# Folding the third hop's weights into the first hop's, and turning its sums on VectorE

## The chip, the core and the metric

The kernel runs on one core of a Trainium2 chip. The metric is device time in microseconds; the time before is the median of three runs. A core has five engines that run side by side, each with its own queue of instructions in order: TensorE (matrix products; PE in the profile, with its weight loads as PEld), VectorE (DVE), ScalarE (ACT), GpSimd (POOL) and SyncE (SP, which here issues the loads). Products land in PSUM banks, and VectorE or ScalarE copies them out.

## The reference

Four layers over one graph of 3327 nodes with 64 features. Each layer takes a layernorm and a relu of `x`, propagates over the dense matrix `adj`, and adds its result to `x`. Cut to what matters:

```
# layer 0: two gated steps                         (hops 0 and 1, adj)
h = relu(layernorm(x));  x = x + L0(h, adj)
# layer 1: out = w @ (h @ weight) + bias           (hop 2, w from the ranks of adj's entries)
h = relu(layernorm(x));  x = x + L1(h, adj)
# layer 2: w = adj * adj                           (hops 3, 4, 5)
h = relu(layernorm(x))
t = h
for W, b in ((W0, b0), (W1, b1), (W2, b2)):
    t = w @ t
    t = t @ W.T + b
x = x + t
# layer 3: twice                                   (hops 6 and 7, adj)
h = relu(layernorm(x));  t = h
for k in range(2):
    t = tanh(concatenate([adj @ t, t], axis=1) @ W[k])
x = x + t
```

## The kernel before, in words

The nodes are padded to 26 blocks of 128, kept as two halves of 13 blocks. The 13 blocks form four chunks (`CH`): chunks 0, 1 and 2 have three blocks (384 columns), chunk 3 has four (512 columns). A chunk stands for its blocks in both halves. Chunks 0 and 1 are group 0, chunks 2 and 3 group 1. A tile is one row block of `adj.T` (128 source nodes) with the columns of one group in both halves; it is loaded by SP into one of 20 slots.

A *unit* (`propagate`, L613) multiplies one tile with the features of its source block, for one destination chunk, and adds to that chunk's sums in PSUM: features stand in the first half of the partitions for the first half of the nodes, in the second for the other. Products in float32 appear as two records each, so that a unit has four.

`joint(g, k, sweep, later, keep)` runs hop k and hop k+1 for group g over the same loaded tiles. First come the tiles whose sources lie in the other group; hop k+1 follows hop k by `later` tiles. Then come the group's own twelve (or fourteen) tiles for hop k alone: all but the last `sweep` for both chunks at a time, then the last `sweep` for the first chunk, then the same ones for the second. When a chunk's sums are complete, its task `after_k` is begun. Then hop k+1 takes the waiting tiles (`keep`), then the tiles whose sources lie in the group's first chunk, for which that chunk's new features must be ready, then those of the second chunk.

Everything is emitted by one Python program in a manual order. The tasks are generators: `yield 1.2` hands back until units of about that many microseconds have been emitted (`spend`). The order of instructions on each engine is the order of emission, and the engines wait for each other's results. If a unit needs features that are not emitted yet (`finish`), the rest of that task is emitted at once.

For hops 3 to 5 the matrix is squared element by element, on ScalarE (L446) or VectorE (L448). `square` gives every third square to VectorE, but none while any chunk's task is open (`ch in tasks`). In hops 3 and 4 the square replaces the tile where it lies. In hop 5 the tile is needed unsquared for hop 6, so `expand` writes the square into half a slot, at most three units ahead of the unit in hand.

Layer 2 in the kernel before: `fold_hops` computes, from the weights in `bd` (index 0 is layer 1's weight, 1 to 3 are W0, W1, W2 transposed, each twice on a block diagonal) and the biases in `brow`, the product of the first two weights (`product(1, 2)`, L214), the first bias carried through the second weight (L241) and the second bias as a column (`hopcol`, L242). Then
- `after_3` copies the sums (`evacuate`, L759 on ScalarE or L761 on VectorE), multiplies with the folded weight (`dense_to_nodes`, recorded at L313, which also turns features into node rows) and adds the folded bias (L1005);
- `after_4` copies the sums with the second bias added (`sums_to_nodes`, L816, ScalarE) and turns them into node rows with VectorE's 32x32 block transposes, sixteen a chunk (L825);
- `after_5` copies the sums, multiplies with W2 (L313), adds the result to `x` (`xs`, L865), takes the layernorm (L843 to L858, with one step on GpSimd at L854) and leaves a feature copy for hop 6 (`transpose_on_vector`, L809);
- the third bias is added to `x` in `after_2`, 15 us after the layernorm (`add_row`, L871).

`after_6` copies the sums into the stacked buffer `both` (`evacuate_stacked`: first half L830 on ScalarE, second half L834 on VectorE), multiplies with layer 3's weights (L780), and ScalarE takes the tanh (L1030).

Of the kernel before, what the change touches and what calls it, by code (L numbers as in the profile page):

```python
# [9 lines left out]
F32 = mybir.dt.float32  # L10
# [3 lines left out]
ALU = mybir.AluOpType  # L14
# [30 lines left out]
N, D = 3327, 64  # L45
P = 128
# [8 lines left out]
CWM = 512  # L55
GROUPS = [(0, 1), (2, 3)]
# [9 lines left out]
WL1, WL2, WL3 = 14, 15, 18  # L66
# [25 lines left out]
def upper(n):  # L92
    return slice(n * D, (n + 1) * D)
# [3 lines left out]
def kernel(  # L97
# [9 lines left out]
    nc = tc.nc  # L107
# [3 lines left out]
    work = ctx.enter_context(tc.tile_pool(name="work", bufs=4))  # L111
# [99 lines left out]
        nc.scalar.copy(ahead[c], ps[:, :width(c)])  # L211
        give(i)

    def product(i, j):  # L214

        n, ps = take()
        mm(ps[:, :P], bd[:, i, :], ident)
        tr = work.tile([P, P], F32, name="t2")
        nc.scalar.copy(tr, ps[:, :P])
        give(n)  # L220
        yield 1.0
        n, ps = take()
        mm(ps[:, :P], tr, bd[:, j, :])
        nc.scalar.copy(bd[:, i, :], ps[:, :P])
        give(n)
        yield 1.0

    def fold_hops():

        i, ps = take()  # L230
        for n in range(3):
            for h in range(2):
                nc.tensor.matmul(ps[upper(h), n * P:(n + 1) * P], brow[:, n], ident, start=True, stop=True)
        cols = work.tile([P, CWM], F32, name="t2")
        nc.scalar.copy(cols[:, :3 * P], ps[:, :3 * P])
        give(i)
        yield 1.0

        i, ps = take()
        mm(ps[:, :D], cols[:, :P], bd[:, 2, :D])  # L240
        nc.vector.tensor_copy(brow[:, 0], ps[:, :D])  # L241
        nc.vector.tensor_copy(hopcol[:, 0:1], cols[:, P:P + 1])  # L242
        give(i)
        yield 1.0
        yield from product(1, 2)

    def more_constants():
        nc.gpsimd.memset(cells, 0.0)
# [59 lines left out]
    def mm(out, lhsT, rhs, start=True, stop=True):  # L308


        for h in range(2):
            hs = slice(h * D, (h + 1) * D)
            nc.tensor.matmul(out[hs], lhsT[:, hs], rhs, start=start, stop=stop)  # L313
# [8 lines left out]
    def take(sums=False, either=True):  # L322


        either = either and not sums
        pool = idle_sums if sums else idle_temps
        if either and idle_sums and (not pool or released[idle_sums[0]] < released[pool[0]]):
            pool = idle_sums
        for c in list(tasks):
            if not pool and c not in running:  # L330
                advance(c)
        i = pool.popleft()
        return i, banks[i]

    def give(i):
        released[i] = max(released) + 1
        (idle_sums if i < 4 else idle_temps).append(i)

    def nodes(c):

        return feat.tile([P, blocks(c), 2, D], F32, name=f"y{c}")

    def flat(t):
        return t.rearrange("p b s d -> p b (s d)")
# [4 lines left out]
    def xchunk(c):  # L349
        return xs[:, CH[c][0]:CH[c][1]]  # L350
# [21 lines left out]
    def finish(c):  # L372
        while c in tasks:
            advance(c)
# [286 lines left out]
    def joint(g, k, sweep, later, keep, lag=None):  # L661


        a, b = GROUPS[g]
        in_place = KIND[k] != PLAIN and KIND[k + 1] == SQUARED
        early = (KIND[k], KIND[k + 1]) == (PLAIN, RANKED)
        waiting = deque()
        counting = Counting(g, lag)

        def both(t):  # L670
            for c in (a, b):
                put(k, c, t)
            if lag is not None:
                counting.add(t)

        def second(n):
            for _ in range(n):
                if waiting:
                    t = waiting.popleft()
                    for c in (a, b):  # L680
                        put(k + 1, c, t)

        for q in sources_of(*GROUPS[1 - g]):
            t = Tile(q, g, in_place, early)
            both(t)
            waiting.append(t)
            if len(waiting) > later:
                second(1)
        own = [[Tile(q, g, in_place, early) for q in sources_of(c)] for c in (a, b)]
        all_own = own[0] + own[1]  # L690
        for n, t in enumerate(all_own[:-sweep]):
            both(t)
            second(len(waiting) + n + 1 > later if early else min(2, len(waiting) - keep))
        counting.rest()
        for c in (a, b):
            for t in all_own[-sweep:]:
                put(k, c, t)
                if lag is not None and c == a:
                    counting.add(t)
            if KIND[k] == RANKED:  # L700
                units.append((k, c, SPECIAL))
        counting.rest()
        second(len(waiting))
        for t in own[0]:
            for c in (a, b):
                put(k + 1, c, t)
        for c in (a, b):
            for t in own[1]:
                put(k + 1, c, t)
            if KIND[k + 1] == RANKED:  # L710
                units.append((k + 1, c, SPECIAL))
# [44 lines left out]
    def evacuate(acc, c, busy=False):  # L756
        m = work.tile([P, CWM], F32, name="t2")[:, :width(c)]
        if c % 2 or busy:
            nc.scalar.copy(m, acc[0][1][:, :width(c)])  # L759
        else:  # L760
            nc.vector.tensor_copy(m, acc[0][1][:, :width(c)])  # L761
        give(acc[0][0])
        return m

    def dense_to_nodes(ft, w, c):

        i, ps = take()
        v = view(ps, c)
        for b in range(blocks(c)):
            mm(v[:, b, :], ft[:, b * P:(b + 1) * P], bd[:, w - WL1, :])  # L770
        return i, v
# [38 lines left out]
                if q % 2:  # L810
                    yield 1.5

    def sums_to_nodes(acc, c, bias):

        m = work.tile([P, CWM], F32, name="t2")[:, :width(c)]
        nc.scalar.activation(m, acc[0][1][:, :width(c)], AF.Identity, bias=hopcol[:, bias:bias + 1])  # L816
        give(acc[0][0])
        yield 0.8
        v = m.rearrange("p (b q n) -> p b q n", q=4, n=32)
        yk = nodes(c)  # L820
        for s in range(2):
            for f in range(2):
                at = s * D + f * 32
                for q in range(4):
                    nc.vector.transpose(yk[q * 32:(q + 1) * 32, :, s, f * 32:(f + 1) * 32], v[at:at + 32, :, q])  # L825
                yield 1.2
        return yk

    def evacuate_stacked(acc, c, on_scalar=False):
        nc.scalar.copy(both[c][upper(0), 0], acc[0][1][upper(0), :width(c)])  # L830
        if on_scalar:
            nc.scalar.copy(both[c][upper(1), 1], acc[1][1][upper(1), :width(c)])
        else:
            nc.vector.tensor_copy(both[c][upper(1), 1], acc[1][1][upper(1), :width(c)])  # L834
        for i in {acc[0][0], acc[1][0]}:
            give(i)
# [24 lines left out]
    def residual(v, c, relu=False):  # L861
        if relu:
            nc.vector.scalar_tensor_tensor(flat(xchunk(c)), v[1], 0.0, flat(xchunk(c)), op0=ALU.max, op1=ALU.add)
        else:
            nc.vector.tensor_tensor(flat(xchunk(c)), flat(xchunk(c)), v[1], ALU.add)  # L865
        give(v[0])

    def add_row(c, i):

        n = 2 * blocks(c)  # L870
        nc.vector.tensor_tensor(groups(xchunk(c)), groups(xchunk(c)),  # L871
                                brow[:, i:i + 1, :].to_broadcast([P, n, D]), ALU.add)
# [113 lines left out]
    def after_2(c, acc):  # L986
        m = evacuate(acc, c)
        yield 1.4
        v = dense_to_nodes(m, WL1, c)
        yield 1.2  # L990
        residual(v, c)
        yk = nodes(c)
        yield from layernorm_relu(yk, c, squares_on_scalar=c in GROUPS[0])
        y[3][c] = yk
        yield 15.0
        add_row(c, 2)

    def after_3(c, acc):
        m = evacuate(acc, c)
# [11 lines left out]
        y[5][c] = yield from sums_to_nodes(acc, c, 0)  # L1011

    def after_5(c, acc):
        m = evacuate(acc, c)
        yield 0.8
        v = dense_to_nodes(m, WL2 + 2, c)
        yield 0.8
        residual(v, c)
        yk = nodes(c)
        yield from layernorm_relu(yk, c)  # L1020
        y[6][c] = yk
        yield 8.0
        yield from transpose_on_vector(yk, c)

    def after_6(c, acc):
        evacuate_stacked(acc, c)
        yield 1.3
        v = stacked_to_nodes(c, lambda s: w3[:, 0, s])
        yk = nodes(c)
        nc.scalar.activation(flat(yk), v[1], AF.Tanh)  # L1030
        give(v[0])
        y[7][c] = yk
        yield 8.0
        yield from transpose_on_vector(yk, c)
# [20 lines left out]
    joint(1, 2, sweep=6, later=6, keep=1)  # L1055
    joint(0, 3, sweep=8, later=4, keep=4)
    joint(1, 4, sweep=8, later=4, keep=4)
    joint(0, 5, sweep=8, later=4, keep=4)
    joint(1, 6, sweep=8, later=4, keep=4)
    alone(0, 7, sweep=6, parts=True)  # L1060

# [55 lines left out]
```

## Time and profile before

| | |
|---|---|
| median of three runs | 697.64 us (697.54 to 697.74) |
| the profiled execution's own time | 697.73 us |
| its span in the profile | 695.7 us |
| instructions in it | 12589 |
| GpSimd busy | 77.8 us (11%) |
| loads and stores | 201.31 MB, mean 289 GB/s |
| mean granted TensorE clock | 0.999 |

Engine shares name the busy time of each engine, its share of the span and its instructions. A group of instructions has the line, the engine, the operation, what it writes and reads, and the count. In the list of waits a row says who waited for whom: microseconds in total, times, the longest. The chain of waits is the work that ended last, followed back from the end. In the timeline a row has start, duration, engine and line; the bracket gives the idle time before it and what ended that.

### The profile page before, as it was taken

The numbers are of one execution on the slowest core, as the hardware profiler recorded it, in microseconds if no ns is written. First come the engines' busy times: TensorE is split into PE (matmuls) and PEld (weight loads), VectorE is DVE, ScalarE is ACT, GpSimd is POOL, SyncE is SP. The second block draws the span as 40 slices with busy tenths as digits, with TensorE's granted clock in tenths as the row PEclk, the third lists the DMA queues.
The fourth block names the chain that finished last, engine by engine and source line by source line (L and its number), as shares of the span: only waits on it lengthen the run. The fifth ranks groups of instructions, "written<-read, shape, count | busy, mean of one in ns | idle before, by whom it ended". The sixth has DMA issues, their size and how long they took to land.

```text
span 695.7 us, 12589 instructions
## 1 busy us (share of the span) xinstructions
PE 681.0 (98%) x5072; PEld 380.4 (55%) x5072; DVE 355.3 (51%) x772; ACT 274.3 (39%) x426; POOL 77.8 (11%) x114
## 2 busy tenths in 40 slices
PE   7899999999999999999999999999999999999997
PEld 4686667645566785556444444343344444344587
DVE  5946745755997899757341106325271565005101
ACT  1013000403147878888998107722176500000101
POOL 5300000002480414111100000000000000000000
PEclk9999999999999999999999999999999999999999
DMA  9999998099879921792899569954997399917991
GB/s 341 401 400 406 403 407 274 1 349 389 277 242 376 317 96 60 259 316 80 311 361 351 206 216 409 404 227 131 396 370 264 110 399 405 405 75 268 404 403 65
DMA packets 68693, 201.31 MB, mean 289 GB/s; under 512 B 7244, under 2 KB 8372, under 8 KB 68636
## 3 DMA queue, kind: packets, MB, share of 16 engines
q1 hardware_dynamic: 65724, 199.08, 76.9%
q10 hardware_dynamic: 736, 1.23, 0.5%
q8 instruction: 40, 0.66, 0.4%
q0 software_dynamic: 2176, 0.20, 0.2%
q14 instruction: 17, 0.14, 0.0%
HBM read 199.45 MB, written 0.85 MB: 288 GB/s over the span
## 4 chain that ended last, share of the span: by engine, by line
PE 58%; DVE 1%; ACT 0%; POOL 0%; issue 0%; DVEq 0%; ACTq 0%; POOLq 0%
PE sum L613 54%; PE temp L313 3%; PE temp L780 1%; ACT e L529 0%; POOL st L854 0%; DVE both L834 0%; DVE e L527 0%; PE sum L313 0%; ACT both L830 0%; DVE y L858 0%; DVE y L850 0%; DVE t L845 0%; DVE st L851 0%; DVE st L843 0%; DVE xs L865 0%
## 5 line engine op out<-in xcount | busy, mean ns | idle before, releaser
L613 PE MATMUL sum<-adj,y 128*64 128x384 f32 (+3 forms) x3016 | 535.4, 501 | 1.5 <-DVE y L858 0.7
L613 PEld LDWEIGHTS sum<-adj,y 128*64 128x64 f32 x3016 | 248.8, 137 | 230.5 <-issue 196.9
L446 ACT ACTIVATE adj<-adj 128x768 f32<-128x768 f32 (+1 forms) x176 | 144.4, 892 | 45.9 <-PE sum L613 23.0
L472 DVE TENSOR_SCALAR adj<-adj 128x768 bf16<-128x768 f32 (+3 forms) x208 | 114.0, 597 | 32.6 <-PE temp L548 24.7
L613 PE MATMUL sum<-e,both 128*64 128x384 bf16 (+1 forms) x624 | 74.0, 339 | 0.5 <-DVE e L527 0.5
L529 ACT ACTIVATE e<-temp,bitsb 128x384 int16<-128x384 f32 (+1 forms) x120 | 67.8, 607 | 14.9 <-PE temp L313 9.1
L830 ACT COPY both<-sum 64x384 f32<-64x384 f32 (+3 forms) x17 | 8.1, 478 | 148.2 <-PE sum L613 148.2
L834 DVE COPY both<-sum 64x384 f32<-64x384 f32 (+3 forms) x13 | 7.3, 561 | 99.5 <-ACT both L830 98.9
L448 DVE TENSOR_TENSOR adj<-adj 128x768 f32<-128x768 f32 (+1 forms) x32 | 30.6, 1004 | 51.9 <-DMA adj<-in_adjT 33.1
L854 POOL TENSOR_TENSOR st<-st,mhalf 128x6 f32<-128x6 f32 (+1 forms) x16 | 24.9, 1553 | 287.8 <-DVE st L852 287.8
L313 PE MATMUL temp<-adj,tri 128*64 128x384 bf16 (+1 forms) x332 | 51.7, 341 | 1.3 <-ACT e L529 0.8
L613 PEld LDWEIGHTS <-both 128*64 128x64 bf16 x624 | 41.9, 110 | 18.3 <-issue 6.5
L477 POOL DMA_DIRECT2D adj<-totals x52 | 33.6, 648 | 52.6 <-PE temp L313 41.7
L313 PEld LDWEIGHTS <-tri 128*64 128x64 bf16 x416 | 29.2, 110 | 17.3 <-issue 9.8
L527 DVE TENSOR_SCALAR e<-temp 128x384 int16<-128x384 f32 (+1 forms) x46 | 28.3, 615 | 20.0 <-PE temp L313 9.6
L809 DVE STREAM_TRANSPOSE both<-y 32x96 f32<-32x96 f32 (+1 forms) x128 | 35.6, 278 | 2.9
L548 PE MATMUL temp<-adj,behind 128*64 128x384 bf16 x208 | 33.8, 340 | 2.8 <-DVE adj L472 2.6
L825 DVE STREAM_TRANSPOSE y<-t 32x96 f32<-32x96 f32 (+1 forms) x64 | 17.8, 278 | 24.7 <-ACT t L816 23.9
L548 PEld LDWEIGHTS <-behind 128*64 128x64 bf16 x208 | 20.8, 110 | 17.4 <-issue 13.5
L761 DVE COPY t<-sum 128x384 f32<-128x384 f32 x6 | 3.3, 555 | 35.7 <-PE sum L613 35.7
L186 ACT COPY t<-temp 128x128 f32<-128x128 f32 x1 | 0.3, 266 | 48.2 <-PE temp L184 48.2
L570 POOL MEMSET adj<- 128x768 f32 (+1 forms) x2 | 1.6, 800 | 133.2 <-PE sum L613 133.2
(132 smaller groups left out, 353.8 us busy)
## 6 DMA issues: line engine op xcount, KB each, us to landing
adj<-in_adjT SPq DMA_DIRECT2D x130, 768.0 KB, 9.0
adj<-in_adjT SPq DMA_DIRECT2D x104, 896.0 KB, 12.0
xs<-in_x ACTq DMA_DIRECT2D x1, 448.0 KB
adj<-totals POOLq DMA_DIRECT2D x26, 3.0 KB, 4.9
adj<-totals POOLq DMA_DIRECT2D x26, 3.5 KB, 2.3
out<-xs ACTq DMA_DIRECT2D x1, 256.0 KB
xs<-in_x SPq DMA_DIRECT2D x1, 192.0 KB
xs<-in_x ACTq DMA_DIRECT2D x1, 192.0 KB, 3.3
```

The lines of the kernel that those rows point to most:

```text
L313: nc.tensor.matmul(out[hs], lhsT[:, hs], rhs, start=start, stop=stop)
L446: nc.scalar.activation(sq, v, AF.Square)
L448: nc.vector.tensor_tensor(sq, v, v, ALU.mult)
L472: nc.vector.tensor_scalar(t.mask.view[:rows, half], t.view()[:rows, half], 0.0, None, op0=ALU.not_equal)
L477: nc.gpsimd.dma_start(out=t.mask.view[P - 1:P], in_=totals[t.g][t.q:t.q + D + 1:D, :])
L527: nc.vector.tensor_scalar(wide[:, s], ps[:, :w], BITS, 0.0, op0=ALU.add, op1=ALU.max)
L529: nc.scalar.activation(wide[:, s], ps[:, :w], AF.Relu, bias=bitsb)
L548: nc.tensor.matmul(counts[c][1][s * D:(s + 1) * D, :w], behind[:, NQ - 1 - t.q:NQ - 1 - t.q + D], t.mask.view[:, s, t.cols(c)], start=firs ...
L613: nc.tensor.matmul(acc[h][1][h * D:(h + 1) * D, :w], yq[h], rhs[h], start=first and n == 0, stop=last and n == len(terms) - 1)
L809: nc.vector.transpose(to[at:at + 32, :, q], h[q * 32:(q + 1) * 32, :, s, f * 32:(f + 1) * 32])
L825: nc.vector.transpose(yk[q * 32:(q + 1) * 32, :, s, f * 32:(f + 1) * 32], v[at:at + 32, :, q])
L854: nc.gpsimd.tensor_tensor(st[:, 3, :n], st[:, 2, :n], mhalf[:, :n], ALU.pow)
```

## The change

The three weights of layer 2 are folded into one before hop 3. With M the squared matrix, M(M(M h W0' + b0)W1' + b1)W2' + b2 is computed as M(M(M h W0'W1'W2' + b0 W1'W2') + b1 W2') + b2. The fold is done in three steps. After hop 5 the sums are copied with b2 added and turned on VectorE, as after hop 4; the second chunk of a group turns only after the first chunk's layernorm has been emitted (`behind`). `add_row(c, 2)` and the 15 us before it are gone. The `sweep` of hop 5 in group 0 grows from 8 to 12 tiles, and for group 0 both halves of the sums of hop index 6 are copied by ScalarE.

```diff
-    def product(i, j):
-
-        n, ps = take()
-        mm(ps[:, :P], bd[:, i, :], ident)
-        tr = work.tile([P, P], F32, name="t2")
-        nc.scalar.copy(tr, ps[:, :P])
-        give(n)
-        yield 1.0
-        n, ps = take()
-        mm(ps[:, :P], tr, bd[:, j, :])
-        nc.scalar.copy(bd[:, i, :], ps[:, :P])
-        give(n)
-        yield 1.0
-
     def fold_hops():
 
         i, ps = take()
-        for n in range(3):
+        for n, w in enumerate((P, 1, 1)):
             for h in range(2):
-                nc.tensor.matmul(ps[upper(h), n * P:(n + 1) * P], brow[:, n], ident, start=True, stop=True)
-        cols = work.tile([P, CWM], F32, name="t2")
-        nc.scalar.copy(cols[:, :3 * P], ps[:, :3 * P])
+                nc.tensor.matmul(ps[upper(h), (0, P, P + 1)[n]:(0, P, P + 1)[n] + w], brow[:, n], ident[:, :w],
+                                 start=True, stop=True)
+        for n in (1, 2):
+            mm(ps[:, (n + 1) * P:(n + 2) * P], bd[:, n, :], ident)
+        turns = work.tile([P, 4, P], F32, name="t2")
+        nc.scalar.copy(turns[:, 0:3].rearrange("p n f -> p (n f)")[:, :P + 2], ps[:, :P + 2])
+        nc.scalar.copy(turns[:, 2:4], ps[:, 2 * P:].rearrange("p (n f) -> p n f", f=P))
         give(i)
         yield 1.0
-
-        i, ps = take()
-        mm(ps[:, :D], cols[:, :P], bd[:, 2, :D])
-        nc.vector.tensor_copy(brow[:, 0], ps[:, :D])
-        nc.vector.tensor_copy(hopcol[:, 0:1], cols[:, P:P + 1])
+        i, ps = take()
+        mm(ps[:, :P], turns[:, 3], bd[:, 3, :])
+        mm(ps[:, P:P + 1], bd[:, 3, :], turns[:, 1, 0:1])
+        nc.scalar.copy(bd[:, 2, :], ps[:, :P])
+        nc.vector.tensor_copy(hopcol[:, 0:1], ps[:, P:P + 1])
+        nc.vector.tensor_copy(hopcol[:, 1:2], turns[:, 1, 1:2])
         give(i)
         yield 1.0
-        yield from product(1, 2)
+        i, ps = take()
+        mm(ps[:, :P], turns[:, 2], bd[:, 2, :])
+        mm(ps[:, P:P + D], turns[:, 0], bd[:, 2, :D])
+        nc.scalar.copy(bd[:, 1, :], ps[:, :P])
+        nc.vector.tensor_copy(brow[:, 0], ps[:, P:P + D])
+        give(i)
...
-    def sums_to_nodes(acc, c, bias):
+    def sums_to_nodes(acc, c, bias, behind=None):
 
         m = work.tile([P, CWM], F32, name="t2")[:, :width(c)]
         nc.scalar.activation(m, acc[0][1][:, :width(c)], AF.Identity, bias=hopcol[:, bias:bias + 1])
         give(acc[0][0])
         yield 0.8
+        for _ in range(50):
+            if behind in (None, c) or y[6][behind] is not None:
+                break
+            yield 0.3
+        else:
+            finish(behind)
...
         y[3][c] = yk
-        yield 15.0
-        add_row(c, 2)
...
     def after_5(c, acc):
-        m = evacuate(acc, c)
-        yield 0.8
-        v = dense_to_nodes(m, WL2 + 2, c)
-        yield 0.8
-        residual(v, c)
-        yk = nodes(c)
+        yk = yield from sums_to_nodes(acc, c, 1, behind=GROUPS[c // 2][0])
+        nc.vector.tensor_tensor(flat(xchunk(c)), flat(xchunk(c)), flat(yk), ALU.add)
         yield from layernorm_relu(yk, c)
...
     def after_6(c, acc):
-        evacuate_stacked(acc, c)
+        evacuate_stacked(acc, c, on_scalar=c in GROUPS[0])
...
-    joint(0, 5, sweep=8, later=4, keep=4)
+    joint(0, 5, sweep=12, later=4, keep=4)
```

## The prediction

> **What bounds the kernel now.** I read the engine shares first, then TensorE's waits, then the chain of waits, then the queues of ScalarE and VectorE beside the edited places.
>
> ```profile
> PE 681.0 (98%) x5072; PEld 380.4 (55%) x5072; DVE 355.3 (51%) x772; ACT 274.3 (39%) x426; POOL 77.8 (11%) x114
> ...
> PE temp L176 <- DMA xs<-in_x: 3.9, 1, 3.9
> PE temp L548 <- DVE adj L472: 2.6, 4, 1.3
> PE temp L313 <- ACT e L529: 0.8, 2, 0.6
> ```
>
> TensorE is busy for 681.0 of 695.7 us. Its named waits come to about 10 us, and all but tenths of them lie before 335 us: from there to 656 us it never stands still for a measurable time. So in hops three to seven an instruction taken off TensorE is worth its full length, and a result that reaches TensorE late costs its full delay. The chain of waits around the ends of hop five shows both the price of the removed products and how dense the neighbourhood is:
>
> ```profile
> 497.61 0.68 PE temp L313 x12
> 498.29 7.30 PE sum L613 x36
> 505.59 0.87 PE temp L313 x16
> 506.46 41.28 PE sum L613 x256
> 547.74 0.66 PE temp L313 x12
> 548.39 5.16 PE sum L613 x32
> 553.55 0.66 PE temp L313 x12
> ```
>
> L313 here is hop five's product with W2; each row ends where the next begins, so nothing hides them. The L613 rows give the clock of everything below: 256 records are 64 units (one tile and one chunk each) of width 384, 41.28/64 = 0.645 us a unit; a 512-wide one takes 0.86 us.
>
> [...] 16 turns of 32x96 take 4.54 us (below), the product that they replace 0.66 us. But TensorE has no free time here and VectorE is idle half of it, so I go by the row of waits: the exchange pays if 4.5 us more latency stay covered. [...] ScalarE: 39% over the span, but 13.17 of 17 us between 536 and 553 us, where hop five of group 0 runs alone. There I judge by the stretch, not by the page's average.
>
> **Part 1: products of hop five removed.** 0.68 + 0.87 + 0.66 + 0.66 = 2.87 us of TensorE, all on the path. Gain 2.87.
>
> **Part 2: weights folded.** At 160 us the old fold put ten 128-column products, two 64-column ones, and nothing else on TensorE: 0.65 + 0.11 + 0.22 + 0.22 = 1.20 us (how much later each following row starts). The new one has the same ten and two, and six one-column products, 12 records; the narrowest row, 64 columns at L780, is 0.70/24 = 0.029 us a record, so about 0.3 us (bounds 0 and 0.4). ScalarE now has a copy (new L231) that waits for the second step's product ahead of the tanh at L915, which ran at 161.43. It slips to about 163.3, and L919 on VectorE from 163.18 to about 163.9; the turn on TensorE that needs this comes at 172.31, so 6 us of cover hide it. Its SP and POOL queues are unchanged. Cost 0.3.
>
> **Part 3: bias row of hop two gone.** Four VectorE additions of 0.55 to 0.68 us, and the 15 us for which the chunk's task stayed open. While a task is open, the rule in `square` sends all squares to ScalarE; by the instruction order five squares near 341 us now go to VectorE (about 1 us each, VectorE idle from 341.1 to 348.7), and leave ScalarE, which is full there. TensorE did not wait there, so worth 0.
>
> **Part 4: ScalarE squares of hop five, group 0.** This is the cost I expect. The longer tasks of chunk 3 and chunk 0 keep the rule on ScalarE: of the 24 units of hop five that run with no other hop between them, VectorE squared six and now squares two, and ScalarE takes four more and the evacuation of chunk 0 (0.48 us). Before:
>
> ```profile
> 534.93 3.04 ACT L446 ACTIVATE adj<-adj 128x768 f32<-128x768 f32 x4 [1.65 <-issue]
> 538.16 2.31 ACT L446 ACTIVATE adj<-adj 128x768 f32<-128x768 f32 x3 [0.18 <-ACT adj L446]
> 541.38 3.04 ACT L446 ACTIVATE adj<-adj 128x768 f32<-128x768 f32 x4 [0.91 <-ACT adj L446]
> 545.25 5.47 ACT L446 ACTIVATE adj<-adj 128x768 f32<-128x768 f32 x7 [0.83 <-ACT adj L446]
> 552.31 0.48 ACT L759 COPY t<-sum 128x384 f32<-128x384 f32 x1 [1.59 <-PE sum L613]
> ```
>
> Squares follow each other at (3.04-0.83)/3 = 0.74 to (5.47-0.83)/6 = 0.77 us; TensorE eats one in 0.645. Four half slots hold results, so a square can be at most four units ahead: a run starts with about 0.5 us in hand and loses 0.10 to 0.12 a unit. Counting unit 0 as the first: units 0 to 10 are squared by ScalarE, 11 by VectorE, 12 and 13 by ScalarE, 14 by VectorE, then the evacuation (it waits for unit 11's sum) and units 15 to 23. At 0.74 TensorE waits 0.1 us up to unit 10 and 0.3 in the second run, at 0.77 0.4 and 0.5. The same holds once more at the start of hop five's first five tiles (504 us): their squares just kept up behind 0.87 us of W2 products that are now gone; 0.15 to 0.25 us. Together 0.6 to 1.15, I take 0.85.
>
> **Part 5: VectorE's chain from sums to features.** Its rows:
>
> ```profile
> 422.24 9.08 DVE L825 STREAM_TRANSPOSE y<-t 32x96 f32<-32x96 f32 x32 [14.89 <-ACT t L816]
> ...
> 498.33 0.56 DVE L865 TENSOR_TENSOR xs<-xs,temp 128x384 f32<-128x384 f32 x1 [0.98 <-PE temp L313]
> ...
> 503.16 0.56 DVE L858 SCALAR_TENSOR_TENSOR y<-t,st 128x384 f32<-128x384 f32 x1 [1.50 <-POOL st L854]
> ```
>
> So 0.62 us from evacuation to first turn, 9.08/2 = 4.54 for sixteen, and 5.39 from the residual to the end of the layernorm: 10.6 us a chunk. The new wait (`behind`) keeps the second chunk's turns behind the first one's layernorm, so the two chunks run one after the other on VectorE; only hop-six units and feature turns wait behind them.
> - Group 1: chunk 2's sums end at 496.7, features at 507.4; first wanted 6.45 us after chunk 3's end (503.65), at 510.1. Chunk 3, 512 wide: about 520, wanted at 525.6. Covered.
> - Group 0, from the start of unit 0: chunk 0's sums end at 8.1, features at 18.8; wanted at the end of unit 23 (24 x 0.645 = 15.5, and about 0.4 to 0.9 of part 4's waits: 15.9) plus eight units, 15.9 + 5.2 = 21.1. The sweep of 12 instead of 8 puts twelve units between the two ends. Chunk 1 queues behind: turns 18.8 to 23.4, features at 28.8; wanted twenty units after unit 23's end, 15.9 + 12.9 = 28.8. No slack: it costs 0 to 0.5, and I take 0, because whatever ScalarE delays at unit 23 also moves this due time.
> - Then 32 feature turns (0.30 us each by the 20 in 5.99 us at 560.02): chunk 0's done at 32.4 and wanted at 34, chunk 1's at 37 and wanted at 39.
>
> **Part 6: second half of group 0's stacked sums copied by ScalarE** (hop index 6). ScalarE is idle there, two copies of 0.48 us end as early as the old pair (569.74 to 570.80), and the copy would otherwise queue behind those turns. Worth 0; without it up to 3 us.
>
> **Sum.** -2.87 + 0.3 + 0 + 0.85 + 0 = -1.7 us. The profiled execution took 697.73 us, 2.03 outside its span, which stay; the median is 697.64, 0.09 below it. 697.64 - 1.7 = **695.9 us**. Loads stay as they are: SP waits mostly for freed slots, which come earlier with TensorE.
>
> **Rivals.**
> 1. *Covers hold everywhere.* The squares keep up (ScalarE's start is earlier than I reckon, or its waits on TensorE are shorter). For: no wait on ScalarE shows anywhere after 335 us. Against: 0.74 is over 0.645. Then -2.87 + 0.3 gives 695.1.
> 2. *Eaten up.* ScalarE at the upper pace (1.15), chunk 1 late by 0.5, fold at 0.4, and 0.2 from the renumbered PSUM banks in hop two, whose buffers rotate differently after the fold: -0.6, 697.0. For: every term is inside its bounds; against: all at once.
> 3. *Slower: the serial VectorE chain of group 0 becomes the path.* Its 21 us have no slack for chunk 1, and every microsecond more is paid in full by TensorE. If turns and layernorms run 20% slower beside ScalarE's traffic than in the rows above, it is 4.2 us late: 697.64 - 1.7 + 4.2 = 700.1. It decides against the change beyond 1.7 us of delay. Against it: 32 turns held 0.284 us while ScalarE squared without a pause (422 to 431 us).
>
> That the change doesn't do what it says can be excluded: the built order shows the 52 products gone and the 64 turns there.
>
> **Numbers.** The measurement can tell about 0.2%, 1.4 us, from no change, so faster means below 696.24. Forecast 0.50, rival 1 0.22, rival 2 0.20, rival 3 0.08. The forecast's own spread, 695.3 to 696.6, lies about four fifths below that bound: faster 0.40 + 0.22 = 0.62, same 0.10 + 0.20 = 0.30, slower 0.08. The range leaves out rival 3 and reaches past 1 and 2 by the unknown in hop two: 694.5 to 697.5.
>
> **What would show it.** No L313 rows at the ends of hop five, TensorE's busy time about 2.6 us less, ScalarE nearly without gaps for 15 us before the end of group 0's hop five, with small TensorE waits on L446's squares, about 0.1 us a unit, and the layernorm of chunk 1 ending within 0.5 us of TensorE's need of it. I am wrong if those waits are absent (rival 1), or if TensorE waits over 1 us for a layernorm's last row near 565 us (rival 3).

## The result, and the profile after

The changed kernel takes 699.91 us (median of 6 runs, 699.84 to 699.99), beside 697.64 us (697.54 to 697.91) of the kernel before on the same chip: 2.27 us more, a ratio of 1.0032 with an interval of 1.0019 to 1.0045. The span of its profiled execution is 698.1 us, 2.4 us longer. The forecast was 695.9 and faster.

Line numbers after `fold_hops` have moved: the units of L613 are now at L609, ScalarE's squares of L446 at L442 (VectorE's of L448 at L444), the first step of the gates on VectorE (L919) at L921, VectorE's turns of L825 at L827, the feature turns of L809 at L805, the last step of the layernorm (L858) at L860, the stacked products of L780 at L776.

Engine shares on the page of the changed kernel:

```profile
PE 680.3 (97%) x5032; PEld 387.7 (56%) x5032; DVE 370.7 (53%) x831; ACT 274.5 (39%) x429; POOL 76.7 (11%) x114
```

Its list of TensorE's waits (microseconds in total, times, longest):

```profile
...
PE temp L776 <- DVE both L805: 1.4, 2, 0.8
...
PE temp L896 <- DVE both L836: 0.7, 1, 0.7
...
PE sum L609 <- ACT e L525: 0.5, 1, 0.5
```

TensorE has forty records fewer and 0.7 us less busy time, and the span is longer all the same. Three waits are new: on the feature turns (L805), on a copy of the gates (L836), and on a mask of hop two (L525). The wait on the last step of the layernorm also grew, from 0.7 to 1.3 us, but at the start of the kernel, and without effect: the first product of the fold stands at 160.16 in both traces. The timeline of TensorE puts the new waits in their places:

```profile
167.29 1.02 PE L896 MATMUL temp<-both,cells 128*64 128x512 f32 x2
169.02 3.22 PE L896 MATMUL temp<-both,cells 128*64 128x512 f32 x13 [0.70 <-DVE both L836]
...
180.67 1.15 PE L309 MATMUL sum<-ident,adj 128*64 128x64 f32 x32 [0.21 <-DVE adj L923]
...
202.68 0.68 PE L609 MATMUL sum<-e,both 128*64 128x384 bf16 x6 [0.51 <-ACT e L525]
...
544.80 27.34 PE L609 MATMUL sum<-adj,y 128*64 128x384 f32 x166
571.96 0.28 PE L776 MATMUL temp<-w,both 128*64 128x64 f32 x4
572.83 0.30 PE L776 MATMUL temp<-w,both 128*64 128x64 f32 x2 [0.58 <-DVE both L805]
573.94 0.74 PE L776 MATMUL temp<-w,both 128*64 128x64 f32 x17 [0.81 <-DVE both L805]
...
574.57 3.60 PE L609 MATMUL sum<-adj,y 128*64 128x384 f32 x19
```

In the kernel before, the gate products and the turn behind them have these rows:

```profile
166.94 2.97 PE L894 MATMUL temp<-both,cells 128*64 128x512 f32 x12
...
178.87 1.15 PE L313 MATMUL temp<-ident,adj 128*64 128x64 f32 x32 [0.31 <-DVE adj L921]
```

The 27.34 us row is what was hoped for: where the kernel before had two rows of hop five's product, the units now run on without one. I followed how far each row lies behind its counterpart before:

| place | later by | what is added there |
|---|---|---|
| first gate products after the fold could start (167.29, before 166.94) | 0.35 | the fold's one-column products |
| the turn that follows the gates (180.67, before 178.87) | 1.80 | 1.45: VectorE's queue at the fold |
| gate products beside the start of hop two (209.33, before 206.88) | 2.45 | 0.65: a wait in hop two |
| hop five, from chunk 2's evacuation (499.28) to chunk 1's (553.48) | | 54.20, before 55.51 (496.80 to 552.31) with 2.21 of W2 products in it: 53.30 without. +0.90 for the squares, -2.21 |
| chunk 1's W2 product, right after that stretch | | -0.66 |
| the wait at L776 | | +1.9 |

The last: from ScalarE's copy of hop six's sums for chunk 0 (570.25, before 569.74) to the row of units after the stacked products (574.57, before 572.15) it is 4.32 us, and 2.41 before. The sum is -2.87 + 0.35 + 1.45 + 0.65 + 0.90 + 1.9 = 2.38, and the spans differ by 2.4. These sizes come from one trace each; the experiments below take them one at a time.

ScalarE in hop five of group 0, which answers to the five rows of before:

```profile
535.55 9.64 ACT L442 ACTIVATE adj<-adj 128x768 f32<-128x768 f32 x13 [1.00 <-ACT adj L442]
545.34 0.58 ACT L812 ACTIVATE t<-sum,hopcol 128x384 f32<-128x384 f32 x1
545.82 6.69 ACT L442 ACTIVATE adj<-adj 128x768 f32<-128x768 f32 x9
553.48 0.58 ACT L812 ACTIVATE t<-sum,hopcol 128x384 f32<-128x384 f32 x1 [0.97 <-PE sum L609]
```

Twenty-two squares with only the evacuation between them, and hardly a gap: ScalarE is the pace here, at 0.74 us a square. And VectorE's chain for chunk 0 and chunk 1, with the turns that follow:

```profile
545.95 4.52 DVE L827 STREAM_TRANSPOSE y<-t 32x96 f32<-32x96 f32 x16 [0.25 <-ACT t L812]
...
555.34 0.56 DVE L860 SCALAR_TENSOR_TENSOR y<-t,st 128x384 f32<-128x384 f32 x1 [1.50 <-POOL st L856]
555.81 4.51 DVE L827 STREAM_TRANSPOSE y<-t 32x96 f32<-32x96 f32 x16
...
563.72 1.12 DVE L805 STREAM_TRANSPOSE both<-y 32x96 f32<-32x96 f32 x4
565.19 0.56 DVE L860 SCALAR_TENSOR_TENSOR y<-t,st 128x384 f32<-128x384 f32 x1 [0.35 <-POOL st L856]
565.78 8.10 DVE L805 STREAM_TRANSPOSE both<-y 32x96 f32<-32x96 f32 x28
```

Chunk 1's features end at 565.75. They are due twenty units after chunk 1's sums, whose end is put at 0.1 us before ScalarE's copy at 553.48. That is an estimate of 553.38 + 12.9 = 566.28: 0.5 us to spare, and TensorE does not wait for them. The loss is in the last row. A timeline row adds up a line's instructions whatever tile they write. By VectorE's instructions in the built program, in their order, the 4 and the 28 turns are:

```
L805 StreamTranspose      both0 <- y0   x4
L860 TensorScalarPtr      y1    <- ...
L805 StreamTranspose      both1 <- y1   x16
L805 StreamTranspose      both0 <- y0   x12
```

Twelve of chunk 0's sixteen turns stand behind all of chunk 1's, and end at 573.88. Chunk 0's stacked products want them at 571.96.

### The profile page after: what moved, and what is told of

Read it like the earlier page. It is cut to its first block, busy times and chain, and to the rows that moved or that the text cites. A ratio compares the mean times of both kernels' runs of the same rounds, so it can differ in the third digit from the quotient of the medians.

```text
span 698.1 us, 12568 instructions
## 1 busy us (share of the span) xinstructions
PE 680.3 (97%) x5032; PEld 387.7 (56%) x5032; DVE 370.7 (53%) x831; ACT 274.5 (39%) x429; POOL 76.7 (11%) x114
## 4 chain that ended last, share of the span: by engine, by line
PE 54%; DVE 4%; ACT 1%; POOL 0%; issue 0%; POOLq 0%; DVEq 0%; ACTq 0%
PE sum L609 51%; PE temp L309 2%; DVE y L827 1%; DVE both L805 1%; PE temp L776 1%; POOL st L856 0%; ACT e L525 0%; DVE t L847 0%; DVE y L852 0%; DVE y L860 0%; DVE st L845 0%; DVE st L853 0%; POOLq L1108 0%; DVE xs L1015 0%; DVE both L836 0%
## 5 line engine op out<-in xcount | busy, mean ns | idle before, releaser
L609 PE MATMUL sum<-adj,y 128*64 128x384 f32 (+3 forms) x3016 | 536.2, 501 | 2.3 <-DVE y L860 1.3
L609 PEld LDWEIGHTS sum<-adj,y 128*64 128x64 f32 x3016 | 259.8, 137 | 223.4 <-issue 179.6
L442 ACT ACTIVATE adj<-adj 128x768 f32<-128x768 f32 (+1 forms) x174 | 142.0, 889 | 22.5 <-DMA adj<-in_adjT 11.9
L609 PE MATMUL sum<-e,both 128*64 128x384 bf16 (+1 forms) x624 | 73.8, 339 | 1.0 <-ACT e L525 0.5
L525 ACT ACTIVATE e<-temp,bitsb 128x384 int16<-128x384 f32 (+1 forms) x120 | 67.9, 607 | 15.4 <-PE temp L309 9.5
L444 DVE TENSOR_TENSOR adj<-adj 128x768 f32<-128x768 f32 (+1 forms) x34 | 32.9, 1016 | 47.7 <-DMA adj<-in_adjT 32.9
L836 DVE COPY both<-sum 64x384 f32<-64x384 f32 (+3 forms) x11 | 6.2, 561 | 96.9 <-ACT both L832 96.4
L827 DVE STREAM_TRANSPOSE y<-t 32x96 f32<-32x96 f32 (+1 forms) x128 | 35.6, 278 | 41.0 <-ACT t L812 39.3
L609 PEld LDWEIGHTS <-both 128*64 128x64 bf16 x624 | 41.7, 110 | 19.2 <-issue 7.6
L805 DVE STREAM_TRANSPOSE both<-y 32x96 f32<-32x96 f32 (+1 forms) x128 | 35.6, 278 | 4.1 <-ACT y L1026 2.2
L812 ACT ACTIVATE t<-sum,hopcol 128x384 f32<-128x384 f32 (+1 forms) x8 | 4.9, 607 | 51.7 <-PE sum L609 51.6
L896 PE MATMUL temp<-both,cells 128*64 128x384 f32 (+1 forms) x72 | 17.2, 525 | 0.7 <-DVE both L836 0.7
```

Of the source, the lines that this page charges most:

```text
L442: nc.scalar.activation(sq, v, AF.Square)
L444: nc.vector.tensor_tensor(sq, v, v, ALU.mult)
L525: nc.scalar.activation(wide[:, s], ps[:, :w], AF.Relu, bias=bitsb)
L609: nc.tensor.matmul(acc[h][1][h * D:(h + 1) * D, :w], yq[h], rhs[h], start=first and n == 0, stop=last and n == len(terms) - 1)
L805: nc.vector.transpose(to[at:at + 32, :, q], h[q * 32:(q + 1) * 32, :, s, f * 32:(f + 1) * 32])
```

## The experiments

The theory after the result (A): the forecast's own terms are right, and three losses were missed: VectorE's queue at the fold, the order of the feature turns, and the bank rotation in hop two. The rival (B) differs by experiment. Times of the kernel before, on the same chip as each group of runs, were 697.76 (697.44 to 698.02, 37 runs) for the first four, 697.69 (697.34 to 698.38, 48 runs) for the next four, and 697.69 (697.46 to 699.08, 31 runs) for the last two.

### The fold alone

The kernel before with the new `fold_hops` put in place of the old one, and nothing else of the change.

```diff
-        for n in range(3):
+        for n, w in enumerate((P, 1, 1)):
...
+        nc.vector.tensor_copy(hopcol[:, 0:1], ps[:, P:P + 1])
+        nc.vector.tensor_copy(hopcol[:, 1:2], turns[:, 1, 1:2])
...
+        nc.vector.tensor_copy(brow[:, 0], ps[:, P:P + D])
```

> The kernel before with the new three-step fold alone; everything behind it is as before, so layer 2's second weight enters twice and its third bias as before (the values differ, the work is the same). Theory A (the fold costs: six one-column products 0.3 us, VectorE's bias copies waiting ahead of a gate chain 1.4 us, and a changed rotation of PSUM banks at the start of hop two 0.7 us): 699.7 to 700.2 us, with a TensorE wait for VectorE's copy of stacked sums near 169 us. Rival B (the fold is hidden, all of the loss is in hop five's VectorE chain): 697.7 to 698.1.

Measured: 700.59 us (700.31 to 700.82), 2.83 us above the kernel before (ratio 1.0042, 1.0027 to 1.0057). Both waits of the changed kernel are there and nothing else of it is, in the timeline of TensorE:

```profile
160.48 0.59 PE L219 MATMUL temp<-ident,brow 128*64 128x128 f32 x12
...
169.34 3.22 PE L890 MATMUL temp<-both,cells 128*64 128x512 f32 x13 [0.70 <-DVE both L830]
...
203.00 0.68 PE L609 MATMUL sum<-e,both 128*64 128x384 bf16 x6 [0.51 <-ACT e L525]
```

So a handful of small instructions at 160 us, which the prediction put at 0.3, cost nearly as much as the removed products bring. The 2.83 is some 0.4 above the table's 0.35 + 1.45 + 0.65. In the profiled execution, which took 700.82, 0.3 of this was there before the fold did anything: its first product stands at 160.48, and at 160.16 in the kernel before. That part isn't the fold's; the other three runs left no trace, and how much of their time it is stays open.

### The fold's three small copies on ScalarE

```diff
-        nc.vector.tensor_copy(hopcol[:, 0:1], ps[:, P:P + 1])
-        nc.vector.tensor_copy(hopcol[:, 1:2], turns[:, 1, 1:2])
+        nc.scalar.copy(hopcol[:, 0:1], ps[:, P:P + 1])
+        nc.scalar.copy(hopcol[:, 1:2], turns[:, 1, 1:2])
...
-        nc.vector.tensor_copy(brow[:, 0], ps[:, P:P + D])
+        nc.scalar.copy(brow[:, 0], ps[:, P:P + D])
```

> The changed kernel with the three small copies of the fold (two bias columns, one bias row) on ScalarE instead of VectorE, nothing else moved. Theory A: the wait of 0.7 us near 169 us goes, the gate chain of chunk 2 is early again: 698.5 to 699.0 us (0.9 to 1.4 less than the changed kernel). Rival B: 699.7 to 700.1, as the changed kernel.

Measured: 698.83 us (698.63 to 699.08), 1.2 us better than the changed kernel, each against its own runs of before. VectorE at the fold, in the kernel before:

```profile
162.88 0.22 DVE L241 COPY brow<-sum 128x64 f32<-128x64 f32 x1 [2.66 <-PE sum L313]
163.03 0.14 DVE L242 COPY hopcol<-t 128x1 f32<-128x1 f32 x1
163.18 1.12 DVE L919 TENSOR_TENSOR adj<-both,adj 64x384 f32<-64x384 f32 x2
...
166.37 0.69 DVE L834 COPY both<-sum 64x512 f32<-64x512 f32 x1 [0.88 <-ACT both L830]
```

in the changed kernel:

```profile
163.59 0.16 DVE L232 COPY hopcol<-sum 128x1 f32<-128x1 f32 x1 [3.36 <-ACT bd L231]
163.66 0.14 DVE L233 COPY hopcol<-t 128x1 f32<-128x1 f32 x1
165.69 0.22 DVE L240 COPY brow<-sum 128x64 f32<-128x64 f32 x1 [1.89 <-ACT bd L239]
165.93 1.12 DVE L921 TENSOR_TENSOR adj<-both,adj 64x384 f32<-64x384 f32 x2
...
168.27 0.69 DVE L836 COPY both<-sum 64x512 f32<-64x512 f32 x1
```

and then in this experiment:

```profile
164.29 1.12 DVE L921 TENSOR_TENSOR adj<-both,adj 64x384 f32<-64x384 f32 x2 [4.02 <-ACT adj L917]
...
166.93 0.69 DVE L836 COPY both<-sum 64x512 f32<-64x512 f32 x1 [0.34 <-ACT both L832]
```

The gates' first step L921 needs ScalarE's tanh, which ends at 164.07 in the changed kernel. (Before, the same step already stood behind two copies of the fold: the tanh ended at 162.05, the step began at 163.18. But that delay was taken up by the 0.88 us for which VectorE then waited ahead of L834.) In the changed kernel it starts at 165.93, because L240 stands ahead of it and waits for the third step of the fold. L240 itself takes 0.22 us. Behind L921 stands the copy L836, and for that TensorE waits. With the copies on ScalarE L836 is 1.34 us earlier and the wait of 0.70 at TensorE is gone. Theory A holds; the wait in hop two is untouched, as it expected.

### Chunk 0's feature turns ahead of chunk 1's

```diff
-            if y[k][cs] is None:
-                finish(cs)
+            while y[k][cs] is None:
+                advance(cs) if k == 6 else finish(cs)
```

`finish` emits all that is left of a task. Here it is called by the first unit of hop six that needs chunk 1's features, and what is left of chunk 1's task includes its sixteen turns. The edit emits only as far as the features.

> The changed kernel, where a unit of hop index 6 that needs a chunk's features takes the chunk's task only as far as these features, and does not empty it. VectorE's feature turns of chunk 0 then stand ahead of chunk 1's sixteen. Theory A: the products of chunk 0's stacked sums near 572 us no longer wait: 697.9 to 698.2 us (1.7 to 2.0 less than the changed kernel). Rival C (VectorE's two chains in a row are late in themselves, whatever the order of the turns): under 0.4 us less, with the wait moved to chunk 1's products near 578 us.

Measured: 698.07 us (697.79 to 698.19), 1.96 us better than the changed kernel, each against its own runs of before (ratio to before 1.0005, 0.9997 to 1.0014: the loss is nearly gone). The timeline of TensorE has no wait at the stacked products:

```profile
571.93 0.87 PE L776 MATMUL temp<-w,both 128*64 128x64 f32 x24
572.63 3.61 PE L609 MATMUL sum<-adj,y 128*64 128x384 f32 x20
```

Units go on 1.94 us sooner than in the changed kernel, with the same instructions on every engine.

### Both together

> e2 and e3 together. Theory A, the two costs lying 400 us apart on TensorE's path: they add, 696.5 to 697.1 us. Rival D (a wait taken away early only makes the later one longer): no better than the better of the two alone, 697.9 or more.

Measured: 696.97 us (696.80 to 697.18), ratio 0.9990 (0.9981 to 0.9998). Against before that is -0.79; the two gains, 1.2 and 1.96, add up to the 3.06 between this and the changed kernel, within a tenth. The stretch of hop five stays at 54.20 us (498.14 to 552.34). The next four experiments stand on this kernel.

### Chunk 0's squares on VectorE

The rule in `square` is set aside for chunk 0 in hop five's own run: five squares on VectorE instead of two.

```diff
-    def square(sq, v, turn):
-        if turn % 3 or any(ch in tasks or (2, ch) in sums for ch in range(NC)):
+    def square(sq, v, turn, own=False):
+        if turn % 3 or (not own and any(ch in tasks or (2, ch) in sums for ch in range(NC))):
...
-            square(wide, t.view(c), t.q + c)
+            square(wide, t.view(c), t.q + c, own=c == 0 and t.q % NB < CH[2][0])
```

> e4_both, with every third square of chunk 0 in group 0's own run of hop five given to VectorE whatever chains are open there: five squares on VectorE instead of two, all of them ahead of chunk 0's turns in VectorE's queue. Theory A (the stretch from chunk 2's hop-five end to chunk 1's, 54.20 us against 53.30 before, is longer by ScalarE's extra squares, the first 0.1 to 0.4 of it in chunk 0's run): the stretch comes to 53.8-54.1, the time to 696.5-696.9 (e4_both was 696.97). Rival B (the 0.9 has nothing to do with ScalarE's squares): the stretch stays at 54.20 and the time at 696.9-697.1.

Measured: 696.72 us (696.56 to 696.97), 0.18 below the last kernel, each against its own before; the stretch is 54.04 us (498.04 to 552.08). Both lie in A's ranges. The times of the two kernels overlap at the edges, but the waits do not. TensorE's weight loads wait for squares; between 535 and 545 us, with these squares on ScalarE (the kernel with both mends):

```profile
PEld sum L609 <- ACT adj L442: 2.6, 8, 0.5
```

and here:

```profile
PEld sum L609 <- DVE adj L444: 0.4, 2, 0.3
PEld sum L609 <- ACT adj L442: 0.4, 2, 0.2
```

Here the waits of weight loads lay mostly beside a running product: 2.6 us of them shrink to 0.8, and the stretch to the end of the hop gets 0.16 shorter. No TensorE product has a named wait on a square in the changed kernel, so its own list of waits does not show this loss; it shows in the weight loads and in the length of the stretch.

### Chunk 1's squares too

```diff
-            square(wide, t.view(c), t.q + c, own=c == 0 and t.q % NB < CH[2][0])
+            square(wide, t.view(c), t.q + c, own=c < 2 and t.q % NB < CH[2][0])
```

> As e5_chunk0_squares_vector, but for chunk 1 too: eight squares of group 0's hop five on VectorE, as in the kernel before; three of them fall among chunk 0's turns there. Theory A: ScalarE's 0.9 us is gone (stretch 53.3), but VectorE's chain gets three times 0.96 us longer and chunk 1's features, which had 0.5 us to spare, come 2 to 3 us late: TensorE waits for the last residual add, 697.5-699. Rival B (VectorE's chain has time to spare that the due time of 566.3 does not show): 695.9-696.3, the best of all.

Measured: 699.40 us (699.25 to 699.59), 2.50 us worse than with both mends, 0.4 above the upper end that A gave. One part of A's text was wrong: the stretch does not shrink to 53.3, it is 54.45 us (497.97 to 552.42). The three squares stand among chunk 0's turns in VectorE's queue, and TensorE waits for them between 545 and 554 us:

```profile
PEld sum L609 <- DVE adj L444: 1.7, 2, 1.3
...
PE sum L609 <- DVE adj L444: 0.6, 1, 0.6
```

The rest is as A had it: the layernorm of chunk 1 ends at 567.23, and TensorE waits 1.88 us for it at 567.29. Rival B is out: VectorE has no room for these squares here. So 0.74 us of the 0.90 are put down to ScalarE's squares by the trace alone, not by an experiment that took them away. The rows of the changed kernel say where they fall. In chunk 1's run, from the copy at 545.34 to the one at 553.48, twelve units take 8.14 us, where twelve times 0.645 are 7.74: 0.40. For the hop's first tiles these two rows of the same squares, before and after, show it:

```profile
513.65 1.58 ACT L446 ACTIVATE adj<-adj 128x768 f32<-128x768 f32 x2 [1.00 <-ACT adj L446]
514.91 1.58 ACT L442 ACTIVATE adj<-adj 128x768 f32<-128x768 f32 x2 [1.08 <-PE sum L609]
```

The changed kernel is 2.48 us late at chunk 2's evacuation and 1.26 late here. Of the 1.55 us of W2 products that are gone in between, it keeps 1.22: 0.33 lost. Outside 535 to 545 us weight loads wait 6.9 us for squares, and 0.9 before.

### A sweep of eight again

```diff
-    joint(0, 5, sweep=12, later=4, keep=4)
+    joint(0, 5, sweep=8, later=4, keep=4)
```

> e4_both with TensorE sweeping 8 blocks of chunk 1 instead of 12 before it evacuates chunk 0 sums' successors in the joint hop of group 0, so that less TensorE work stands between the end of hop five and the first product that needs chunk 1's features. Theory A (those features come 0.5 us before they are due, so the cover has nothing to give): the features are 2.1 to 2.6 us late, 698.5-699.5. Rival B (the cover is much longer than the features need): 696.8-697.2, no difference.

Measured: 699.21 us (699.10 to 699.40), 2.31 us worse than with both mends. (The text's "8 blocks of chunk 1" are the tiles that chunk 0's sums get ahead of chunk 1's.) Chunk 0's turns start at 547.26 instead of 544.81, chunk 1's features end at 567.04, and TensorE waits for them:

```profile
567.10 6.03 PE L609 MATMUL sum<-adj,y 128*64 128x384 f32 x36 [1.88 <-DVE y L860]
```

With a second wait of 0.28 on chunk 0's features at 557.25 that is 2.16 of the 2.31. The due time that the prediction worked out is real, and the chain had the half microsecond that the trace shows and no more.

### The PSUM banks of before

Each tile of PSUM goes into the next free bank. The old fold takes and returns a bank four times, the new one three times, so every later tile sits one bank further. The edit takes and returns one more, with no instruction on it.

```diff
+        yield 1.0
+        give(take()[0])
```

> e4_both with one PSUM bank taken and given back after the fold, with no instruction on it, so that every later tile sits in the bank it had in the kernel before. Theory A (the wait of 0.51 us on ScalarE's evacuation at the start of hop two, and 0.65-0.7 us of the shift there, come from the renumbered banks): the wait is gone and the time is 696.2-696.5. Rival B (it comes from the fold's shift in time against the evacuations): the wait stays and the time is 696.9-697.1.

Measured: 696.39 us (696.11 to 696.76), 0.51 below the kernel with both mends, each against its own before. Of the wait of 0.51 on L525 nothing is left in TensorE's timeline there (L611 and L311 are the same lines, two further down):

```profile
200.61 0.91 PE L611 MATMUL sum<-e,both 128*64 128x384 bf16 x6
201.23 0.62 PE L311 MATMUL temp<-adj,tri 128*64 128x384 bf16 x4
```

An edit without an instruction gains half a microsecond: theory A holds, the loss is the rotation and not the shift in time.

### All four mends

> All four mends together: the fold's small copies on ScalarE, chunk 0's feature turns ahead of chunk 1's, the PSUM bank given away after the fold, chunk 0's squares of hop five on VectorE. If they are separate losses (theory A), e4_both's 696.97 less 0.58 for the bank and 0.25 for the squares: 695.9-696.3, with what is left of the change being 2.87 taken away, 0.35 for the fold's one-column products and 0.6 for chunk 1's squares on ScalarE. If one mend's gain is only a wait that another also removes (rival B), 696.4-696.7.

Measured: 696.21 us (696.07 to 696.37), ratio 0.9977 (0.9968 to 0.9985). That is 1.48 us faster than the kernel before and the fastest kernel of this study. Against the kernel with both mends it is 0.69 better, the 0.51 of the banks and the 0.18 of the squares: the losses are separate.

### The second stacked copy on VectorE again

The kernel with all four mends, with one part of the change undone.

```diff
-        evacuate_stacked(acc, c, on_scalar=c in GROUPS[0])
+        evacuate_stacked(acc, c)
```

> e9_four_mends with one part of the change undone: the second stacked half of group 0 in hop seven is copied by VectorE again. Theory A (the prediction's: both copies are off the path that sets the end, or covered, either way): the same time as e9_four_mends within 0.2. Rival B (the copy on VectorE stands behind the feature turns of hop seven there, and the move is worth something): 0.3-1.0 slower than e9_four_mends.

Measured: 696.85 us (696.67 to 697.57), 0.64 worse: theory A falls, rival B is right. (The text counts the hop from one; it is hop index 6. And what it calls the prediction's is not what Part 6 says, which had VectorE's copy queue behind the turns, as rival B has it.) VectorE:

```profile
569.57 0.56 DVE L838 COPY both<-sum 64x384 f32<-64x384 f32 x1 [1.46 <-ACT both L834]
570.17 4.78 DVE L807 STREAM_TRANSPOSE both<-y 32x96 f32<-32x96 f32 x16
574.97 0.56 DVE L838 COPY both<-sum 64x384 f32<-64x384 f32 x1
```

and TensorE:

```profile
575.59 0.80 PE L778 MATMUL temp<-w,both 128*64 128x64 f32 x20 [0.38 <-DVE both L838]
```

The second copy starts the moment that sixteen turns ahead of it are done, and the stacked products wait for it. The profiled execution here is itself the longest of the runs (697.57); 0.8 of its span is a wait for the first tiles at the start, so only rows next to each other are read from it.

## Why the prediction was wrong

The forecast was -1.7 us, the result is +2.27; the spans, on which the sum is made, differ by 2.4. Step by step:

**Right.** Part 1: the products are gone and by the rows bring their 2.87 us. In Part 2 the one-column products were put at 0.3 and cost 0.35. In Part 3 five squares did move to VectorE, and TensorE gained nothing: its lag is 2.45 us at 209 and 2.48 at 499. Part 4 took 0.85 for ScalarE's squares, and the stretch is longer by 0.90. By its three places: the first run was to cost 0.1 to 0.4, and taking its squares away brought 0.16 to 0.18; the second was to cost 0.3 to 0.5, and by the rows costs 0.40; the first tiles were to cost 0.15 to 0.25, and by the rows cost 0.33. (The 0.1 does not follow from the figures beside it: 0.10 a unit over eleven units, less the 0.5 us in hand, leaves a wait of about 0.6. That the first run's figure fits is luck, as far as its working shows.) In Part 5 group 1 was covered, chunk 1's features came 0.5 us before their due time, and rival 3, the layernorm that comes too late, did not happen; the sweep of eight and chunk 1's squares on VectorE each show what it costs once it does. Sixteen turns take 4.52 us beside ScalarE's full row of squares (at 545.95), and took 4.54 before. The exchange itself went as forecast: 2.87 us of W2 products left TensorE's path, and the 4.5 us of turns that replace them stayed covered up to the features. What the exchange lost in hop six, it lost through the order of what stands behind them in VectorE's queue.

**Signs.** The prediction would have called itself wrong if TensorE had shown no waits on the squares. Its products show none; the waits are in the list of its weight loads, and the experiment on chunk 0's squares shows that they cost time. TensorE's busy time was to fall by about 2.6 us and fell by 0.7, though the products are gone. Of the time lost, at least the 0.90 of hop five is counted as busy, as the rows of the products have no gap there. And the 699.91 lies near rival 3's 700.1 by chance, as the layernorm for which that rival let TensorE wait came in time.

**Wrong: Part 2, "it slips to about 163.3, and L919 on VectorE from 163.18 to about 163.9 ... 6 us of cover hide it".** ScalarE's slip was right: the tanh starts at 163.45. Not counted were VectorE's own three copies, which are emitted ahead of L919 (L921 in the changed kernel). The first waits for the second step of the fold, as the old copies did (162.88); the last now waits for the third step, and runs 2.1 us after the first (165.69 against 163.59). The trace shows what that does to VectorE's queue: L921, emitted behind L240, is held to 165.93 for operands that were there at 164.07. And the cover was measured to the wrong reader. The turn at 172 is not the first to need VectorE: the copy L836 stands behind L921 to L923 in the same queue, and TensorE's gate products need that at 167.3 (their row of two at 167.29, and then the wait). Cost 1.45 by the traces where 0 was set down; the experiment that moved the three copies took 1.2 of it away by the time and 1.34 by the trace.

**Wrong: Part 5, "chunk 0's done at 32.4 and wanted at 34".** This took the 32 feature turns to run chunk 0 first. The code says otherwise: `finish` empties chunk 1's task when hop six first wants its features, and four of chunk 0's turns had been emitted by then. Chunk 0's are done at 573.88, about 36.6 on the prediction's clock. Cost 1.9 where 0 was set down. The sum of VectorE's work was right, and its order was not looked up.

**Wrong in size: rival 2's "0.2 from the renumbered PSUM banks".** It was named, but outside the forecast, and it measured 0.51 by the run and 0.65 by the traces.

**Right: Part 6.** It kept VectorE's copy out from behind the feature turns, and put that at nothing beside the kernel before. With the copy on VectorE again the mended kernel is 0.64 us slower, and the copy does stand behind sixteen turns. The "up to 3 us" is a bound; in the kernel without the mends it was not measured.

The two wrong steps cost 1.45 + 1.9 us and the banks 0.65; without them the forecast's terms give -2.87 + 0.35 + 0.90 = -1.62, and with the banks, 0.16 of the squares and the two queues mended the kernel measures -1.48. The 0.3 between that and -1.62 - 0.16 lies inside the interval of the ratio.

## What to carry to other kernels

When an edit makes an instruction wait for another engine, list what is emitted behind it on its own queue, down to the first result that the bounding engine reads: a copy of 0.22 us, which waited for another engine ahead of the gates' steps, held TensorE back by 1.4 us. Moving work to an idle engine needs the order of that engine's instructions and not only the sum of their durations; a helper that empties a whole task when one result of it is wanted decides that order, and here that cost 1.96 us. Count the buffers that an edit takes and returns: one fewer in a rotation brought a wait of half a microsecond 40 us later.

## What the runs showed of the hardware

- TensorE's list of waits of products did not show that ScalarE set the pace in hop five. The weight loads did: 9.5 us of waits on squares, in 24 waits of at most 0.5 us, between 504 and 554 us, beside 0.90 us of time lost. The rows of the products show no gap there: the one from 544.80 to 572.14 runs through while loads wait 3.8 us for squares between 545 and 554. Why waits of loads cost so little was not shown.
- A bank taken and returned without any instruction on it changed the time by 0.51 us, twice: added to the kernel with both mends, and to the one with chunk 0's squares moved. The named wait that goes with it is the one at 202 us.
